# Cross attention's output projection computed in pairs of token tiles from seven block products, and the last unit's later sums taken by TensorE with ones

## The chip, the cores and the metric

One core of one Trainium2 chip runs the whole kernel in one launch. The metric is the device time of that launch in microseconds (us), the median of three runs. TensorE (PE) does the matrix products, VectorE (DVE) and ScalarE (ACT) the elementwise work, GpSimd (POOL) elementwise work in SBUF and some transfers, SyncE (SP) issues most of the transfers.

## The reference, cut to what matters

One block of a perceiver on 16 batches of 64 latent tokens (1024 tokens in all, 1024 wide, float32). Three residual steps follow each other; the change lies at the end of the first.

```python
x = x + xattn(layernorm(x), ctx, ctx, Wq, Wk, Wv, Wo)   # context: 16 x 1024 x 1024
x = x + attn(layernorm(x), wq, bq, wk, bk, wv, bv)      # rotary, no output projection
x = x + ffn(layernorm(x), w_gate, w_up, w_down)         # int4 / int8 / ternary rounding

def xattn(query, key, value, Wq, Wk, Wv, Wo):           # 32 heads of 32, 8 key/value heads
    ...
    scores = einsum('bhqd,bhkd->bhqk', q, k) * 32 ** -0.5
    probs = softmax(scores)
    out = einsum('bhqk,bhkd->bqhd', probs, v).reshape(b, sq, 1024)
    return out @ Wo                                     # 1024 x 1024
```

## The kernel before

**Tiles.** The 1024 tokens are 8 token tiles of 128, tile t holding batches 2t and 2t+1. Almost everything in SBUF lies in one tile, the `arena`; `place(kb, shape)` is a view of it that begins at that kilobyte of each partition, and the same kilobytes serve several tensors one after the other. All engine queues run in the order in which the code emits the work (a manual schedule), so an instruction that waits holds up everything behind it on its engine.

**Cross attention** is 32 units: unit n is batch n // 2 with key/value heads 4g to 4g+3, g = n % 2. A loop over n = 0 to 31 with an inner loop over i = 0 to 3 interleaves the stages of neighbouring units. Called "step (n, i)" below, a step emits in this order:

- `by_key` of unit n+1 (line 696): scores of a quarter of the keys into the two PSUM tiles w0 and w1; ScalarE copies them to SBUF (line 708), VectorE keeps running maxima (lines 712, 715). At i = 3 `reduce` (lines 720 to 727) finds the maxima over keys and `spread` (lines 733, 734) writes them to DRAM and reads them back to all partitions through SP's queue.
- loads on SP's queue that are tied to that step (token tiles x, outputs of earlier batches, weights).
- `fill(2)`: two pieces from the list `fillers`, which hold projection work for TensorE. A second `fill` follows later in the step.
- at i = 1 and 2, `exponentials` of unit n: VectorE subtracts the maxima (line 739, 128x2048), ScalarE takes the exponential (line 740), and `sums` on GpSimd adds up the keys into `acc` (lines 746, 749).
- at i = 0, `values((2, 3))` of unit n-1 (line 758) and `finish` (line 768, four products of `ones` with `acc`, one for each group of 32 columns); at i = 1 its `quotients` on VectorE (lines 777 to 787). At i = 2, `values((0, 1))` of unit n.

In the last pass, n = 31, there is no following unit, and all exponentials and sums of unit 31 are emitted in it.

**The output projection** `project_out(t, h)` (lines 258 and 798) makes one half of 512 columns of one token tile: eight products of 128x128 weights with 512 moving columns into one PSUM bank (a filler has two of them), then one VectorE addition onto the token tile `xs[t]`. There are 16 of these. Tile (4, 0) is filler of step (29, 3), tiles 5, 4, 0 and 1 are fillers of passes 30 and 31, and tiles 2, 3, 6 and 7 follow after the loop, with the normalization `norm2` (lines 179 to 193) and the transposes `transpose2` (lines 296 to 300) of the next attention among them. After that comes `project2`, whose first product is the k projection (line 258, name k).

Outputs of batches 0 to 11 were kept in DRAM (`results`) and are loaded into `outputs[t]` before their projection; those of the last two tiles stay in SBUF, and tile 7 is only complete after unit 31's `quotients`.

`bank(n, name)` names a PSUM bank: 0 and 1 are m0 and m1, 2 is t1.

The order of SP's queue in passes 29 to 31 follows the code: the maxima's write and read of `spread`, then the loads listed after it. A load waits in the queue until its target kilobytes are free, and holds up those behind it.

Of the kernel before, what the change touches and what calls it, by code (L numbers as in the profile page):

```python
# [20 lines left out]
P = 128  # L21
# [28 lines left out]
def kernel(  # L50
# [148 lines left out]
    early = [place(16 * half, [4, 2, 2, 4, NQ]) for half in range(2)]  # L199
    two_tiles = [place(4 * i, [2, 2, 4 * NQ]) for i in range(2)]  # L200
    two_outputs = [place(4 * i, [2, 4, 2, NQ]) for i in range(2)]
    outputs = [place(8 + 4 * t if t < 6 else 4 * (t - 6), [2, 4, P]) for t in range(NT)]

    qa = [place(16 * g, [B * 4 * NQ]) for g in range(2)]
    queries = [a.rearrange("p (b r q) -> p b r q", r=4, q=NQ) for a in qa]
# [23 lines left out]
    def load_x(dst, t):  # L229
        nc.sync.dma_start(dst, x[bass.ts(t, P), :])  # L230

    def load(src):
        st = stream.next([KC, 512])
        nc.sync.dma_start(st, src)
        return st

    def load_half(h, i):
        if i == 0:
            wos.append(stream.next([KC, 512]))
        part = slice(4 * i, 4 * i + 4)  # L240
        nc.sync.dma_start(wos[h][:, part], wo[h][:, part])

    def load_queries(st, src, engine, pieces):

# [5 lines left out]
    def matmul_steps(out, lhsT, rhs, done, pieces=2):  # L250

        made = []

        def piece(i):
            if i == 0:
                made.append(out())
            for k in range(i * KC // pieces, (i + 1) * KC // pieces):
                nc.tensor.matmul(  # L258
                    made[0], lhsT=lhsT(k), rhs=rhs(k), start=(k == 0), stop=(k == KC - 1)
                )  # L260
# [421 lines left out]
    class Unit:  # L682
# [80 lines left out]
                            stop=(kt == 7),  # L763
                        )

        def finish(self):
            for jj in range(4):
                nc.tensor.matmul(
                    self.po[bass.ts(jj, HD), 256:512],
                    lhsT=ones,  # L770
                    rhs=acc[:, jj, :],
                    start=True,
                    stop=True,
                )

        def quotients(self):
            nc.vector.reciprocal(rs, self.po[:, 256:512])
# [9 lines left out]
                nc.gpsimd.tensor_copy(view[:, :, 0, :], split(aside[self.g]))  # L787


    wos = []  # L790

    def project_out(t, h):
        cols = bass.ts(h, 512)
        return matmul_steps(
            lambda: m_tile(f"wo_{t}_{h}"),
            lambda k: outputs[t][:, k // 4, k % 4, :],
            lambda k: wos[h][:, k, :],
            lambda ps: nc.vector.tensor_tensor(xs[t][:, cols], ps, xs[t][:, cols], ALU.add),
            pieces=4,
        )  # L800


    n2T = [[place(kb, [4, 512]) for kb in kbs] for kbs in ((136, 144), (48, 56))]
    n2_ring = Ring(180, 176)
    n2s = {}
    kT2 = place(112, [2, B, NQ])
    v2 = place(120, [NT, KVD])
    oS = place(152, [2, 4, 2, NQ])
    sS = place(156, [4, 2, NQ])

# [5 lines left out]
    turned_ring = Ring(168, 170)  # L816
    rope_sb = place(192.25, [2 * NQ])
    bv_sb = place(192.75, [KVD])
    wkvs2 = place(32, [KC, 512])
    wqs2 = []  # L820
    swap = [(i + HD // 2) % HD for i in range(HD)]

    def norm2(t):
        n2s[t] = n2_ring.next([DIM])
        for step in layernorm(n2s[t], xs[t], f"n2_{t}"):
            step()

    def transpose2(t, tile):
        half, tl = t // 4, t % 4
        cols = bass.ts(tl, P)  # L830
        transposed([a[:, :, cols] for a in n2T[half]], n2s[t], f"n2p_{t}", tile, ("act", "dve"))
# [189 lines left out]
    inter = [  # L1021
        place(kb, [INTER]) for kb in (48, 58.75, 69.5, 80.25, 0, 10.75, 136, 146.75)
    ]
    wb_ring = Ring(32, 34.6875, 37.375, 40.0625, 91.25, 42.75)
    relu_ring = Ring(45.4375, 192.25, 199.625)
    prod_ring = Ring(172.5, 174)
    wds = [place(112 + c if c < 16 else 6 + c, [DIM], F8) for c in range(NIC)]
    q_ring = Ring(157.5, 162.875)
    qT_ring = Ring(48, 59)
    xq3 = {}  # L1030
# [95 lines left out]
    def fetch_down():  # L1126
        wd_rows = ternary_d.rearrange("c p f -> (c p f)").rearrange("(i h) -> i h", h=DIM)
        nc.gpsimd.memset(wds[NIC - 1][LAST:], 0.0)
        for c0, c1 in ((0, 16), (16, NIC - 1)):
            nc.sync.dma_start(  # L1130
                place(112 if c0 == 0 else 22, [c1 - c0, DIM], F8),
                wd_rows[c0 * P : c1 * P].rearrange("(c p) h -> p c h", p=P),
            )
        nc.sync.dma_start(wds[NIC - 1][:LAST], wd_rows[(NIC - 1) * P :])
# [43 lines left out]
    def fill(n=1):  # L1178
        for _ in range(n):
            if fillers:  # L1180
                fillers.pop(0)()

    with tc.manual_schedule():
# [45 lines left out]
        for n in range(2 * B):  # L1229

            b = n // 2
            if n % 2 == 0:
                if n == 2:
                    weight_sum(1, 0)
                fill(len(fillers))
                if b == 0:
                    load_context(1, 1)
                    kT, v, key_steps, value_steps = project(1)
                    for h in range(2):

                        for step in key_steps[h] + value_steps[h]:
                            fillers += [step, lambda: None]
                    begun = project_fast(2)
                    early = begun[2]
                    fillers[-3], fillers[-1] = early[:2]
                    fillers += early[2:]
                elif b + 1 < B:
                    kT, v, early_steps, steps = begun
                    fillers += steps
                    begun = project_fast(b + 2) if b + 2 < B else None  # L1250
                    if begun:
                        fillers += begun[2]
                    else:
                        fillers += project_out(4, 0)
                if b + 1 < B:
                    tiles.append((kT, v))
                else:
                    for t in range(4):
                        load_x(xs[t], t)
                    for t, h in ((5, 0), (4, 1), (5, 1)):  # L1260
                        fillers += project_out(t, h)
                    for t in (0, 1):
                        for h in range(2):
                            fillers += project_out(t, h)
            following = Unit(n + 1, *tiles[(n + 1) // 2]) if n + 1 < 2 * B else None

            for i in range(4):
# [6 lines left out]
                if n == 5 and i == 3:  # L1274
                    nc.vector.tensor_reduce(tot, asum, AX.X, ALU.add)
                if n == 2 * B - 4 and i in (0, 3):
                    load_half(0, i // 3)
                if n == 2 * B - 3 and i == 2:
                    for k in range(2):
                        load_half(1, k)  # L1280
                if i == 1 and n == 2 * B - 2:
                    nc.sync.dma_start(wkvs2, wkv2)

                fast, odd = 1 <= b < B - 1, n % 2
                if n == 0 and i == 3:
# [22 lines left out]
                        nc.sync.dma_start(place(4 * (t % 2), [DIM]), spilled[t + 2])  # L1308
                for when, ts in (
                    ((2 * B - 3, 2), (4, 5)),  # L1310
                    ((2 * B - 3, 3), (2, 3)),
                    ((2 * B - 2, 1), (0, 1)),
                ):
                    for t in ts if when == (n, i) else ():
                        nc.sync.dma_start(outputs[t].rearrange("p g r c -> p (g r c)"), results[t])
# [13 lines left out]
                    unit.sums(1)  # L1329
                if i == 3 and held_back:  # L1330
                    unit.sums(3)
                fill(0 if i == 0 and fast or (n, i) == (6, 2) else 2)
                if i == 1 and held_back:
                    unit.sums(0)
                if last and i == 0:
# [11 lines left out]
                if i == 1 and not following:  # L1347
                    for e in (2, 3):
                        unit.exponentials(e)
                        unit.sums(e)  # L1350
# [4 lines left out]
                if i == 3 and not following:  # L1355
                    unit.values((2, 3))
# [8 lines left out]
        for t in (2, 3):  # L1365
            for h in range(2):
                fillers += project_out(t, h)
                if t == 2:
                    fillers += [lambda h=h: norm2(h)]
            fillers += [lambda t=t: (transpose2(t - 2, m_tile), norm2(t))]  # L1370
        fill(9)
        last.finish()
        last.quotients()
        fill(len(fillers))
        for h in range(2):
            fillers += project_out(6, h)
        fillers += [lambda: transpose2(2, m_tile)]
        for h in range(2):
            fillers += project_out(7, h)
        fill(len(fillers))  # L1380
        transpose2(3, m_tile)
# [189 lines left out]
```

## Time and profile before

| what | number |
| --- | --- |
| median of 3 runs | 1823.31 us (1818.98 to 1824.83) |
| the profiled execution, its own time | 1819.01 us |
| its span in the profile | 1817.2 us |
| mean granted TensorE clock | 0.995 of full speed |
| output projection, line 258 name wo | 256 records, 114.2 us busy |
| the additions of its results, line 798 | 16, 10.9 us busy |

The profile's times are from the start of the span. One float32 product appears as two records of TensorE, so the 256 records are 128 products. A row of the timeline gives the start, the duration, the engine, line, operation, names and shapes, the number of records merged, and in brackets how long the engine was idle before it and who ended that.

### The profile page before, as it was taken

To read this page: it belongs to the slowest core of one execution; us is meant where nothing else is said; L and a number is where in the kernel's file an instruction comes from. 1 tells how busy PE (TensorE), PEld (TensorE's weight loads), DVE (VectorE), ACT (ScalarE), POOL (GpSimd) and SP (SyncE) were. 2 spreads that over 40 slices of the span, in tenths; PEclk is the share of its full clock that TensorE was granted. 3 is DMA by queue.
4 is the path that set the end of the run, shared out by engine and by line. 5 is a ranking of instruction groups with operands and counts; after the bars stand their busy time and mean duration, and the time that the engine had idled before them with its cause. 6 is when DMAs were issued, how large, how long until landed. Compare 5 with 4: busy or idle time off the path is not lost.

```text
span 1817.2 us, 29757 instructions
## 1 busy us (share of the span) xinstructions
PE 1771.3 (97%) x12424; PEld 1139.4 (63%) x12424; DVE 1252.5 (69%) x1500; ACT 946.6 (52%) x1034; POOL 937.7 (52%) x568
## 2 busy tenths in 40 slices
PE   8999999999999999999999999999999998999999
PEld 5887576666667667667667667654346454566654
DVE  4343778778888888878888888877423367675554
ACT  1563666656677777777677665543101122763221
POOL 1000447657767667767767767664403425455510
PEclk9999999999999999999999999999999999999999
DMA  9566457576677777677777766353020022333201
GB/s 355 165 224 216 181 168 210 158 195 192 193 206 198 232 213 208 216 211 205 221 204 215 217 187 168 92 194 143 5 93 0 6 73 63 84 105 112 73 30 53
DMA packets 67735, 285.52 MB, mean 157 GB/s; under 512 B 10576, under 2 KB 19728, under 8 KB 52880
## 3 DMA queue, kind: packets, MB, share of 16 engines
q1 hardware_dynamic: 54288, 213.63, 32.9%
q0 software_dynamic: 12160, 67.89, 18.4%
q8 instruction: 98, 1.61, 0.3%
q10 hardware_dynamic: 1152, 2.10, 0.3%
q14 instruction: 37, 0.30, 0.1%
HBM read 264.38 MB, written 19.20 MB: 156 GB/s over the span
## 4 chain that ended last, share of the span: by engine, by line
PE 83%; DVE 8%; DMA 4%; ACT 3%; POOL 2%; issue 1%; ACTq 0%; DVEq 0%; POOLq 0%
PE p L514 14%; PE p L503 13%; PE t L696 7%; PE o L758 6%; PE q L366 5%; PE q L258 5%; PE wo L258 4%; PE d L1161 4%; PE k L258 4%; PE g L1082 4%; PE gu L1082 3%; DVE arena L739 3%; DMA arena<-in_ctxT 3%; PE z L514 3%; PE v L427 2%; DVE arena L715 2%
## 5 line engine op out<-in xcount | busy, mean ns | idle before, releaser
L749 POOL TENSOR_TENSOR arena<-arena 128x1024 f32<-128x1024 f32 x192 | 506.5, 2638 | 78.5 <-ACT arena L740 63.5
L715 DVE TENSOR_TENSOR arena<-t,arena 128x512 f32<-128x512 f32 x384 | 261.2, 689 | 171.3 <-PE t L696 105.0
L739 DVE TENSOR_TENSOR arena<-arena 128x2048 f32<-128x2048 f32 x128 | 358.8, 2833 | 6.8 <-DMA arena<-tops 6.8
L740 ACT ACTIVATE arena<-arena 128x2048 f32<-128x2048 f32 x128 | 244.1, 1907 | 186.7 <-DVE arena L739 186.5
L514 PEld LDWEIGHTS p<-arena 128*128 128x128 f32 x2688 | 311.5, 193 | 34.0 <-issue 25.7
L708 ACT COPY arena<-t 128x1024 f32<-128x1024 f32 x256 | 253.4, 1009 | 144.5 <-DVE arena L712 62.5
L514 PE MATMUL p<-arena 128*128 128x128 f32 x2688 | 319.7, 277 | 0.0
L503 PE MATMUL p<-arena 128*128 128x512 f32 x672 | 307.5, 599 | 7.3 <-DMA arena<-in_ctxT 7.3
L503 PEld LDWEIGHTS p<-arena 128*128 128x128 f32 x672 | 121.7, 190 | 149.9 <-issue 138.1
L746 POOL TENSOR_TENSOR arena<-arena 128x1024 f32<-128x1024 f32 x32 | 75.6, 2363 | 271.1 <-ACT arena L740 194.5
L696 PE MATMUL t<-arena 32*128 32x256 f32 x2048 | 146.7, 400 | 5.5 <-ACT arena L708 3.3
L1082 PEld LDWEIGHTS <-arena 128*128 128x128 bf16 x1024 | 98.8, 98 | 64.8 <-issue 13.7
L696 PEld LDWEIGHTS t<-arena 32*128 32x128 f32 x2048 | 93.0, 184 | 63.9 <-issue 32.6
L758 PE MATMUL o<-arena 128*32 128x256 f32 x2048 | 124.8, 384 | 4.1 <-ACT arena L740 3.8
L258 PE MATMUL wo<-arena 128*128 128x512 f32 x256 | 114.2, 603 | 0.3 <-ACT arena L298 0.3
L258 PE MATMUL q<-arena 128*128 128x512 f32 x256 | 112.6, 595 | 0.0
L843 POOL TENSOR_TENSOR arena<-arena 128x512 f32<-128x512 f32 x20 | 33.5, 1673 | 133.9 <-DVE arena L841 133.9
L366 PE MATMUL q<-arena 128*128 128x256 f32 x448 | 99.1, 380 | 1.3 <-ACT arena L377 1.3
L758 PEld LDWEIGHTS o<-arena 128*32 128x32 f32 x2048 | 60.3, 110 | 57.5 <-ACT arena L646 6.8
L1082 PE MATMUL gu<-arena 128*128 128x344 fp8e4 x544 | 85.4, 314 | 9.6 <-ACT arena L1090 6.5
L366 PEld LDWEIGHTS q<-arena 128*128 128x128 f32 x448 | 84.2, 190 | 14.4 <-issue 1.7
L483 POOL DMA_DIRECT2D arena<-in_ctxT x70 | 69.4, 1047 | 40.1 <-PE z L514 17.2
(158 smaller groups left out, 2340.0 us busy)
## 6 DMA issues: line engine op xcount, KB each, us to landing
arena<-in_ctxT SPq DMA_DIRECT2D x56, 1024.0 KB, 10.3
arena<-in_ctxT POOLq DMA_DIRECT2D x42, 1024.0 KB, 10.7
arena<-tops SPq DMA_DIRECT2D x48, 512.0 KB, 4.8
arena<-in_wg SPq DMA_DIRECT2D x32, 688.0 KB, 5.1
arena<-in_wu SPq DMA_DIRECT2D x32, 688.0 KB, 5.5
arena<-in_wd SPq DMA_DIRECT2D x32, 688.0 KB, 8.3
arena<-in_ctxT POOLq DMA_DIRECT2D x28, 512.0 KB, 8.4
arena<-ternary POOLq DMA_DIRECT2D x26, 344.0 KB, 3.8
```

What stands on the lines that cost most here:

```text
L258: nc.tensor.matmul(made[0], lhsT=lhsT(k), rhs=rhs(k), start=(k == 0), stop=(k == KC - 1))
L366: nc.tensor.matmul(ps, lhsT=weights[:, k, :], rhs=what[:, k, :], start=(start and k == 0), stop=(k == 3), skip_group_check=True,)
L503: nc.tensor.matmul(ps, lhsT=weights[:, k, :], rhs=what[:, k, :], start=(first and k == 0), stop=(k == 3), skip_group_check=True,)
L514: nc.tensor.matmul(ps[:, bass.ts(kt, P)], lhsT=what[:, k, bass.ts(kt, P)], rhs=weights[:, k, :], start=(first and kt == 0 and k == 0), sto ...
L696: nc.tensor.matmul(ws[jj // 2][:, jj % 2, a, :], lhsT=self.kT[rows, self.g, bass.ts(i * 2 + a, P)], rhs=two_tiles[self.b // 2 % 2][rows, s ...
L708: nc.scalar.copy(pt[:, 2 * mine : 2 * mine + 2], ws[mine])
L715: nc.vector.tensor_tensor(m, w[:, :, a], m, ALU.max)
L739: nc.vector.tensor_tensor(pt, pt, by.to_broadcast([P, 4, 2, 256]), ALU.subtract)
L740: nc.scalar.activation(pt, pt, AF.Exp)
L749: nc.gpsimd.tensor_tensor(acc, acc, pt[:, :, a], ALU.add)
L758: nc.tensor.matmul(self.po[bass.ts(jj, HD), 0:256], lhsT=self.v[:, kt, bass.ts(self.g * 4 + jj, HD)], rhs=self.pts[i][:, jj, a, :], start= ...
L1082: nc.tensor.matmul(ps[:, :CW], lhsT=xqT[t][:, k, :], rhs=wbs[n][i][:, k, :], start=(k == 0), stop=(k == KC - 1),)
```

## The change

Two neighbouring token tiles t and t+1, each cut into two halves of the contraction (512 input rows), make a 2x2 block matrix a11, a12 (tile t) and a21, a22 (tile t+1). `Wo` is a 2x2 block matrix too (`out_blocks`). `project_out(t, turn)` now makes a pair of tiles from seven block products instead of eight. Their operands include sums: `sum_out` makes three sums of weight blocks once (and overwrites b12), `sum_pair` four sums of token blocks for each pair (one overwrites a21), all on VectorE. Four of the products accumulate in one bank (`turn` 0 or 1), one after the other, and after each of them VectorE adds what the bank holds to a quarter of the pair; the other three share bank 2. A filler is two of a product's four matrix products. Pairs go in the order (4, 5), (0, 1), (2, 3), (6, 7).

The last unit's sums of its third and fourth quarter of the keys leave GpSimd; `finish((2, 3))` lets TensorE multiply those probabilities with `ones` and accumulate. Loads move between steps, some tensors move to other kilobytes, the transposes of tiles 0 to 3 use w0 and w1, and step (30, 0) runs two fillers instead of four.

```diff
-    outputs = [place(8 + 4 * t if t < 6 else 4 * (t - 6), [2, 4, P]) for t in range(NT)]
+    outputs = [place(kb, [2, 4, P]) for kb in (8, 12, 196, 24, 24, 28, 0, 4)]
...
-        def finish(self):
+        def finish(self, direct=()):
+            rest = [(i, a) for i in direct for a in range(2)]
             for jj in range(4):
-                nc.tensor.matmul(
-                    self.po[bass.ts(jj, HD), 256:512],
-                    lhsT=ones,
-                    rhs=acc[:, jj, :],
...
+                rows = [acc[:, jj, :]] + [self.pts[i][:, jj, a, :] for i, a in rest]
+                for n, row in enumerate(rows):
+                    nc.tensor.matmul(
+                        self.po[bass.ts(jj, HD), 256:512],
+                        lhsT=ones,
+                        rhs=row,
+                        start=(n == 0),
+                        stop=(n == len(rows) - 1),
+                    )
...
+    def sum_out(n):
+        (b11, b12), (b21, b22) = out_blocks
+        t1, t2, t4 = out_sums
+        out, a, b, op = (
+            (b12, b22, b12, ALU.subtract),
+            (t2, b12, b11, ALU.add),
+            (t1, b22, t2, ALU.subtract),
+            (t4, b21, t2, ALU.subtract),
+        )[n]
+        nc.vector.tensor_tensor(out, a, b, op)
...
+    def sum_pair(t, ns):
+        (a11, a12), (a21, a22) = pair_blocks(t)
+        s1, s2, s4 = pair_sums[t]
+        sums = (
+            (s1, a21, a22, ALU.add),
+            (s2, s1, a11, ALU.subtract),
+            (a21, a11, a21, ALU.subtract),
+            (s4, a12, s2, ALU.subtract),
         )
+        for n in ns:
+            nc.vector.tensor_tensor(*sums[n])
+
+    def project_out(t, turn):
...
+        def product(n, first, what, weights, *adds):
+            def piece(i):
+                if i == 0 and first:
+                    held[n] = bank(n, f"wo_{t}_{n}")
+                for k in (2 * i, 2 * i + 1):
+                    nc.tensor.matmul(
+                        held[n],
...
+                for h, g in adds if i else ():
+                    dst = xs[t + h][:, bass.ts(g, 512)]
+                    nc.vector.tensor_tensor(dst, held[n], dst, ALU.add)
...
+        begin = product(turn, True, a11, b11, (0, 0)) + product(2, True, a12, b21, (0, 0))
+        rest = product(turn, False, s2, t2, (0, 1)) + product(2, True, s1, t1, (1, 1))
+        rest += product(turn, False, s3, t3, (1, 1)) + product(2, False, s4, b22, (0, 1))
+        return begin, rest + product(turn, False, a22, t4, (1, 0))
...
-                        fillers += project_out(4, 0)
+                        pairs = {t: project_out(t, turn % 2) for turn, t in enumerate((4, 0, 2, 6))}
+                        fillers += pairs[4][0]
...
+                    for a, b_ in ((0, 4), (2, 0), (6, 2)):
+                        fillers += pairs[a][0] + pairs[b_][1]
+                    fillers += pairs[6][1]
...
+                if (n, i) == (2 * B - 3, 3):
+                    for t in (0, 1):
+                        load_x(xs[t], t)
+                    sum_out(0)
+                    sum_out(1)
+                if (n, i) == (2 * B - 2, 0):
+                    sum_pair(4, (0, 1))
+                if (n, i) == (2 * B - 2, 1):
+                    sum_out(2)
+                    sum_pair(4, (2,))
+                if (n, i) == (2 * B - 2, 2):
+                    sum_pair(4, (3,))
+                    sum_out(3)
+                if (n, i) == (2 * B - 1, 0):
+                    load_x(xs[2], 2)
+                    sum_pair(0, range(4))
...
                     ((2 * B - 3, 2), (4, 5)),
-                    ((2 * B - 3, 3), (2, 3)),
-                    ((2 * B - 2, 1), (0, 1)),
+                    ((2 * B - 3, 3), (0, 1)),
+                    ((2 * B - 2, 1), (2,)),
+                    ((2 * B - 1, 0), (3,)),
                 ):
                     for t in ts if when == (n, i) else ():
                         nc.sync.dma_start(outputs[t].rearrange("p g r c -> p (g r c)"), results[t])
...
-                fill(0 if i == 0 and fast or (n, i) == (6, 2) else 2)
+                fill(0 if i == 0 and b or (n, i) == (6, 2) else 2)
...
+        load_x(xs[3], 3)
+        sum_pair(2, (0, 1))
+        fill(4)
+        last.values((2, 3))
+        last.finish((2, 3))
+        nc.sync.dma_start(wkvs2, wkv2)
+        last.quotients()
+        sum_pair(2, (2, 3))
+        fill(4)
+        norm2(0)
+        norm2(1)
+        sum_pair(6, range(4))
+        fill(2)
+        transpose2(0, wide_tile)
+        fill(2)
...
```

Below, a block product is named by its operands, for example s1·t1. Emitted into the queues, the fillers fall as follows: step (29, 3) has a11·b11 and a12·b21 of pair (4, 5); step (30, 0) a11·b11 of pair (0, 1); step (30, 1) a12·b21 of pair (0, 1) and s2·t2 of pair (4, 5); step (30, 2) s1·t1 and s3·t3, step (30, 3) s4·b22 and a22·t4, all of pair (4, 5). Pass 31 has a11·b11 (step 0) and a12·b21 of pair (2, 3), then the five later products of pair (0, 1). After the loop come a11·b11 and a12·b21 of pair (6, 7), unit 31's last `values` and `finish`. Ten products remain after `finish`, the five later ones of pairs (2, 3) and (6, 7).

More of the change, by code (lines that the diff above doesn't have):

```diff
@@ L235, in load @@
         return st
[L237 to L241, printed above, removed]
     def load_queries(st, src, engine, pieces):
@@ L764, in values @@
                         )
-        def finish(self):
+        def finish(self, direct=()):
+            rest = [(i, a) for i in direct for a in range(2)]
             for jj in range(4):
-                nc.tensor.matmul(
-                    self.po[bass.ts(jj, HD), 256:512],
-                    lhsT=ones,
-                    rhs=acc[:, jj, :],
-                    start=True,
-                    stop=True,
-                )
+                rows = [acc[:, jj, :]] + [self.pts[i][:, jj, a, :] for i, a in rest]
[7 more added lines that the diff above has]
+                    )
         def quotients(self):
@@ L787, in quotients @@
                 nc.gpsimd.tensor_copy(view[:, :, 0, :], split(aside[self.g]))
[L790 to L799, printed above, removed]
-        )
+    out_blocks = [[place(kb, [4, 512]) for kb in kbs] for kbs in ((64, 16), (72, 32))]
@@ new lines, with load_out @@
+    out_sums = [place(kb, [4, 512]) for kb in (88, 80, 40)]
+    pair_places = {4: (104, 106, 108), 0: (172, 174, 110), 2: (8, 10, 12), 6: (28, 30, 14)}
+    pair_sums = {t: [place(kb, [4, P]) for kb in kbs] for t, kbs in pair_places.items()}
+    def load_out(i, h):
+        nc.sync.dma_start(out_blocks[i][h], wo[h][:, 4 * i : 4 * i + 4])
+    def sum_out(n):
[8 more added lines that the diff above has]
+        nc.vector.tensor_tensor(out, a, b, op)
@@ new lines, in pair_blocks @@
+    def pair_blocks(t):
+        return [[outputs[t + h][:, i] for i in range(2)] for h in range(2)]
+    def sum_pair(t, ns):
[6 more added lines that the diff above has]
+            (s4, a12, s2, ALU.subtract),
+        )
+        for n in ns:
+            nc.vector.tensor_tensor(*sums[n])
+    def project_out(t, turn):
+        (a11, a12), (s3, a22) = pair_blocks(t)
+        s1, s2, s4 = pair_sums[t]
+        (b11, t3), (b21, b22) = out_blocks
+        t1, t2, t4 = out_sums
+        held = {}
+        def product(n, first, what, weights, *adds):
[5 more added lines that the diff above has]
+                        held[n],
+                        lhsT=what[:, k, :],
+                        rhs=weights[:, k, :],
+                        start=(first and k == 0),
+                        stop=(k == 3),
+                        skip_group_check=True,
+                    )
+                for h, g in adds if i else ():
+                    dst = xs[t + h][:, bass.ts(g, 512)]
+                    nc.vector.tensor_tensor(dst, held[n], dst, ALU.add)
+            return [lambda: piece(0), lambda: piece(1)]
+        begin = product(turn, True, a11, b11, (0, 0)) + product(2, True, a12, b21, (0, 0))
+        rest = product(turn, False, s2, t2, (0, 1)) + product(2, True, s1, t1, (1, 1))
+        rest += product(turn, False, s3, t3, (1, 1)) + product(2, False, s4, b22, (0, 1))
+        return begin, rest + product(turn, False, a22, t4, (1, 0))
@@ L805 @@
     n2s = {}
-    kT2 = place(112, [2, B, NQ])
-    v2 = place(120, [NT, KVD])
+    kT2 = place(32, [2, B, NQ])
+    v2 = place(40, [NT, KVD])
     oS = place(152, [2, 4, 2, NQ])
@@ L818 @@
     bv_sb = place(192.75, [KVD])
-    wkvs2 = place(32, [KC, 512])
+    wkvs2 = place(112, [KC, 512])
     wqs2 = []
@@ L1023 @@
     ]
-    wb_ring = Ring(32, 34.6875, 37.375, 40.0625, 91.25, 42.75)
-    relu_ring = Ring(45.4375, 192.25, 199.625)
+    wb_ring = Ring(112, 114.6875, 117.375, 120.0625, 91.25, 122.75)
+    relu_ring = Ring(125.4375, 192.25, 199.625)
     prod_ring = Ring(172.5, 174)
-    wds = [place(112 + c if c < 16 else 6 + c, [DIM], F8) for c in range(NIC)]
+    wds = [place(32 + c if c < 16 else 6 + c, [DIM], F8) for c in range(NIC)]
     q_ring = Ring(157.5, 162.875)
@@ L1130, in fetch_down @@
             nc.sync.dma_start(
-                place(112 if c0 == 0 else 22, [c1 - c0, DIM], F8),
+                place(32 if c0 == 0 else 22, [c1 - c0, DIM], F8),
                 wd_rows[c0 * P : c1 * P].rearrange("(c p) h -> p c h", p=P),
@@ L1257 @@
                 else:
[L1258 to L1264, printed above, removed]
+                    for a, b_ in ((0, 4), (2, 0), (6, 2)):
+                        fillers += pairs[a][0] + pairs[b_][1]
+                    fillers += pairs[6][1]
             following = Unit(n + 1, *tiles[(n + 1) // 2]) if n + 1 < 2 * B else None
@@ L1276 @@
                 if n == 2 * B - 4 and i in (0, 3):
[L1277 to L1282, printed above, removed]
+                    load_out(i // 3, 0)
+                if n == 2 * B - 3 and i in (0, 1):
+                    load_out(1 - i, 1)
+                if (n, i) == (2 * B - 3, 3):
[14 more added lines that the diff above has]
+                    sum_pair(0, range(4))
                 fast, odd = 1 <= b < B - 1, n % 2
@@ L1349 @@
                         unit.exponentials(e)
-                        unit.sums(e)
                 if (n, i) == (6, 2):
@@ L1354 @@
                     unit.values((0, 1))
-                if i == 3 and not following:
-                    unit.values((2, 3))
             if n == 2 * B - 4:
@@ L1363, with wide_tile @@
             last, unit = unit, following
-        fill(len(fillers))
[L1365 to L1381, printed above, removed]
+        def wide_tile(name):
+            turns["m"] ^= 1
+            w = ps_w.tile([P, 2, 2, 256], F32, tag=f"w{turns['m']}", name=name)
+            return w.rearrange("p a b c -> p (a b c)")[:, 0:512]
+        load_x(xs[3], 3)
[13 more added lines that the diff above has]
+        fill(2)
+        transpose2(1, wide_tile)
+        fill(2)
+        norm2(2)
+        fill(2)
+        norm2(3)
+        fill(2)
+        transpose2(2, wide_tile)
+        fill(2)
+        transpose2(3, wide_tile)
+        fill(len(fillers))
         nc.sync.dma_start(rope_sb, rope)
```

## The prediction

> **What bounds the kernel now.** I read the page first, then the chain of waits, then the timelines of TensorE, VectorE and SP around the projection.
>
> ```profile
> PE 1771.3 (97%) x12424; PEld 1139.4 (63%) x12424; DVE 1252.5 (69%) x1500; ACT 946.6 (52%) x1034; POOL 937.7 (52%) x568
> ```
>
> TensorE is the bound of the whole, but an average says nothing on this stage. The chain of waits there:
>
> ```profile
> 1217.35 7.06 PE wo L258 x16
> ...
> 1227.79 7.08 PE wo L258 x16
> 1234.89 0.69 DVE arena L798
> 1235.58 3.81 DVE arena L739
> ...
> 1259.45 1.33 DMA tops<-arena
> 1260.80 4.20 DMA arena<-tops
> ```
>
> In pass 30 the chain changes from TensorE to VectorE and to the maxima's transfer and back: VectorE is within a microsecond or two of being the bound itself. The work of each engine by window (PE, PEld, DVE, ACT, POOL busy, then TensorE's granted clock) says the same:
>
> ```profile
> 1226.00:1262.00 36.00, 36.00 (x200) 16.36 (x190) 28.64 (x29) 13.40 (x10) 17.13 (x7) 1.00 0.35 145
> 1262.00:1300.00 38.00, 34.23 (x132) 14.63 (x128) 19.38 (x14) 7.66 (x4) 21.69 (x10) 0.91 0.12 41
> ```
>
> In pass 30 (first row) TensorE has no gap and VectorE 7.4 us free. TensorE's timeline:
>
> ```profile
> 1217.28 7.13 PE L258 MATMUL wo<-arena 128*128 128x512 f32 x16
> 1224.35 1.93 PE L758 MATMUL o<-arena 128*32 128x256 f32 x32
> 1226.10 0.61 PE L768 MATMUL o<-arena,ones 128*32 128x256 f32 x8
> ...
> 1262.09 14.00 PE L258 MATMUL wo<-arena 128*128 128x512 f32 x32
> ...
> 1282.79 1.94 PE L758 MATMUL o<-arena 128*32 128x256 f32 x16 [3.25 <-ACT arena L740]
> 1284.66 15.78 PE L258 MATMUL wo<-arena 128*128 128x512 f32 x32
> ```
>
> The one long wait (3.25) is for the last exponential. After it the same 32 records take 15.78 instead of 14.00, where the window's clock is 0.91: a long wait costs 1.8 us more behind it. SP and VectorE:
>
> ```profile
> 1219.94 0.33 SPq L734 DMA_DIRECT2D arena<-tops  x1
> ...
> 1221.27 2.25 SPq L230 DMA_DIRECT2D arena<-in_x  x4
> ```
>
> ```profile
> arena<-in_x SPq DMA_DIRECT2D x1, 512.0 KB, 6.8
> ```
>
> The second fence is the DMA view of the transfer issued at 1221.27, the fourth of 512 KB from 1219.94 on: it landed 6.8 later, at 1228.1.
>
> ```profile
> 1265.09 4.49 DVE L739 TENSOR_TENSOR arena<-arena 128x2048 f32<-128x2048 f32 x2 [4.47 <-DMA arena<-tops]
> ...
> 1272.23 8.57 DVE L739 TENSOR_TENSOR arena<-arena 128x2048 f32<-128x2048 f32 x2
> ```
>
> Two such subtractions take 4.49 when GpSimd is idle, 8.57 while it adds: whichever comes second stands still until the other is done.
>
> **Part 1, fewer products.** Before: 8 tiles x 2 halves x 8 = 128. After: 4 pairs x 7 x 4 = 112. 32 records (16 products) take 14.00, so 16 fewer save 14.0 us, all on TensorE's path.
>
> **Part 2, `finish` of unit 31.** 4 products with ones become 20. Below: groups of four in four column groups take 0.61 (row L768), five groups 3.05. Above: one 128x256 product after another (line 366, 99.1 us for 224) is 0.442 each, 20 make 8.8. The new order has five products in a row on the same 32 columns and the same PSUM rows, so I go by line 366 and, as row L768 has different groups side by side, let the last of one group run beside the first of the next: 17 x 0.442 = 7.5, +6.9 over the 0.6 before.
>
> The Trainium skill ("TensorE: Matmul & The Clock Gate", Part 3, packing small matmuls) says that products run side by side when they are in different column groups and that they start and end in order, which speaks against this order; no row here shows five in one group. By that rule the sum stands as it is, by row L768 it would be 4.5 us lower.
>
> The four GpSimd additions that go (2.35 each) ran from 1281.0 to 1290.6, and `finish` came at 1300.4 without a wait: nothing on the path.
>
> **Part 3, the new waits.** I walked the queues by hand from step (29, 3): an instruction starts when its engine is free and its inputs are there, with durations from the rows (additions from PSUM 0.69, 128x512 sums in SBUF 0.69 as line 346, 128x2048 sums 2.28 as line 739, more where GpSimd is in the way). The same walk over the order before puts the first k product at 1348.4; the trace has 1348.25.
>
> - Step (30, 0): TensorE reaches a11·b11 of pair (0, 1) at 1217.3 (by_key begins at 1216.2, as now). Its operand, tile 0's outputs, is loaded behind `spread` and tiles xs[0] and xs[1] on SP. `spread` can't go before the maxima are reduced (1218.5), so the load is issued at 1221.3, fourth behind the broadcast, and lands at 1228.1 as the row above did. Wait 10.8 us. Before, tile 5 stood here, loaded 20 us earlier. Queued behind it: unit 29's last values and `finish`, and the next by_key. VectorE makes the first two weight sums meanwhile (4.6 us, from 1218.4), which the wait hides; without it they would hold by_key up by 3.5.
> - Step (30, 3): s4·b22 needs bank 2, so the addition of s1·t1, which stands on VectorE behind s4's sum and the fourth weight sum. VectorE is through with the maxima at 1252.9, loses 2.2 to GpSimd, and ends s4's sum at 1255.8, the weight sum at 1258.2, the addition at 1258.8. TensorE was free at 1254.9: 3.9 us.
> - Step (31, 0): a11·b11 of pair (2, 3) takes over bank 0 from pair (4, 5). The bank's last addition is emitted after `reduce`, which begins after the last maxima (1268.2) and ends at 1271.9; then two additions to 1273.2. TensorE was free at 1267.6: 5.6 us.
> - VectorE's addition of that product goes onto xs[2], whose load SP issues behind the broadcast, xs[6] and xs[7], landing about 8.2 after the broadcast's issue (4.2, then 1.3 for each of three, 0.1 for the order): 1281.5. The subtraction behind it waits 4 us longer than for the broadcast itself; the four products ahead on TensorE cover it. But later, at step (31, 3), s4·b22 of pair (0, 1) wants bank 2, whose addition stands behind two subtractions slowed by GpSimd (3.4 and 4.5): 1299.3 against 1296.9, 2.4 us.
> - a11·b11 of pair (6, 7) takes bank 1 from pair (0, 1): 0.9. Tiles 0 and 1 transposed: 0.4 for the norm, 1.7 because the copy stands behind sum_pair of (6, 7) and an addition.
>
> Together 10.8 + 3.9 + 5.6 + 2.4 + 0.9 + 0.4 + 1.7 = 25.7. The first three waits are longer than 3 us, so each gets 1.8 of slow clock: 5.3.
>
> **Part 4, what goes.** Waits of 0.5 and 3.3 for the last exponentials (now ten us of products lie between), 1.3 before transposes, 1.8 of slow clock: 6.9.
>
> **What costs nothing.** The sums of weights and tokens not named above, and 28 instead of 16 additions (12 x 0.69 = 8.3), fall into VectorE's gaps; in pass 30 there is no such cover, and that is where the waits come from. wkv is issued behind `finish` (1323.6), 10.4 us to land as now, needed at 1365; were the cover gone, the k product would wait. xs[3] lands at 1308, needed at 1330. The second attention's weights stand behind wkv on SP and have 30 us of k and v products as cover.
>
> **Sum.** -14.0 + 6.9 + 25.7 + 5.3 - 6.9 = +17.0 us. On the profiled execution, 1819.0 + 17.0 = 1836.0; on the median, which is 4.3 above it, 1840.3. I take the middle, 1838. This measurement can tell 0.3%, 5.5 us, from no change. Between the two bases (1821.2) the cases are:
>
> **The rivals.**
> - *TensorE runs through* (faster): VectorE's additions and sums fit its gaps, so that no bank is handed over late and tile 0 is there in time. Place: the bank hand-overs of passes 30 and 31. Price: -14.0 + 6.9 - 6.9 = -14, about 1807. It decides as soon as the new waits and slow clock stay under 14 us against my 31. For it: 69% average use of VectorE. Against: 7.4 free in pass 30, into which more than 15 go. 0.06.
> - *Tile 0's outputs land in time*: the walk without that wait has by_key of step (30, 1) held 3.5 by the weight sums, bank 0 at (31, 0) 7.3, and ends at +10: 1831. Against: the 1228.1 of the row. 0.10.
> - *`finish` runs four abreast*: 3.05 instead of 7.5: +12.5, 1834. 0.15.
> - *VectorE falls further behind*, each short sum held once by a GpSimd addition (2.4) and the clock slow after every wait: +6 on top, 1844. 0.08.
> - Parts cancel within 0.3%: 0.03. That the change isn't what it says I exclude: the queues hold 28 block products and 20 products with ones.
>
> **How the numbers follow.** My forecast has 0.58. With `finish` from 3.05 to 8.8 (-4.5, +1.3), slow clock from none to four times (some 1.7 either way) and the base from 1819.0 to 1824.8 it reaches from 1830 to 1846; the second to fourth rival lie in 1828 to 1847, which leaves out the first, the fifth and some of the tails, under 0.2. Faster 0.06, same 0.03, slower 0.91.
>
> **What would show it.** In the timeline after: TensorE waiting about 10.8 us for `results` after by_key of step (30, 0); waits for VectorE's addition of an earlier product of some 4 and 6 us in steps (30, 3) and (31, 0); a row of 40 records with ones of about 7.5 us; k starting 17 us later than 1348; nothing different after that. Wrong if the first wait is under 3 us, or if k starts before 1350.

## The result and the profile after

The changed kernel takes 1842.2 us (median, 1840.81 to 1843.57) against 1822.07 for the kernel before on the same chip: slower by 1.1%, ratio 1.0111 [1.0092, 1.013] (in brackets its 95% interval). The profiled execution took 1840.81 us, its span is 1839.0 us, 21.8 more than the span of before.

The page of the changed kernel, busy time of each engine:

```profile
PE 1770.3 (96%) x12424; PEld 1139.7 (62%) x12424; DVE 1276.8 (69%) x1532; ACT 945.8 (51%) x1034; POOL 926.2 (50%) x564
```

TensorE is busy 1.0 us less than before, VectorE 24.3 more, while the span is 21.8 longer. So most of what the saved products take off TensorE comes back on it as something else (the products with ones and a lower clock, below), and the added time is TensorE waiting. The number of TensorE records is the same by coincidence (32 fewer of `wo`, 32 more with `ones`). The two windows that the prediction read, now in the changed kernel (columns as there: PE, PEld, DVE, ACT, POOL busy, granted clock, DMA share, GB/s):

```profile
1226.00:1262.00 36.00, 29.74 (x164) 13.63 (x165) 28.74 (x28) 9.34 (x8) 8.14 (x3) 0.88 0.12 50
1262.00:1300.00 38.00, 29.69 (x126) 12.71 (x125) 29.59 (x30) 11.68 (x8) 22.34 (x9) 0.94 0.20 70
```

Where TensorE had no gap in pass 30 it now stands for 6.3 us, and 8.3 in the next window; the longest wait, which ends at 1228.79, lies mostly ahead of the first. The chain of waits has the three that count, the first two by what ended them, the third by the products that stand behind it:

```profile
1221.98 6.76 DMA arena<-results
1228.79 5.48 PE wo L833 x8
...
1254.25 4.36 DVE arena L804
...
1273.61 5.26 PE wo L833 x8
```

L804 is `sum_out`. TensorE's timeline, the rows behind a wait, the row of the last unit's products with ones, and the first k product:

```profile
1228.79 5.48 PE L833 MATMUL wo<-arena 128*128 128x512 f32 x8 [11.05 <-DMA arena<-results]
...
1259.26 8.83 PE L833 MATMUL wo<-arena 128*128 128x512 f32 x16 [3.47 <-DVE arena L843]
1273.61 5.26 PE L833 MATMUL wo<-arena 128*128 128x512 f32 x8 [5.52 <-DVE arena L843]
...
1299.75 8.83 PE L833 MATMUL wo<-arena 128*128 128x512 f32 x16 [2.79 <-DVE arena L843]
1309.36 7.13 PE L833 MATMUL wo<-arena 128*128 128x512 f32 x16 [0.78 <-DVE arena L843]
1318.18 6.30 PE L765 MATMUL o<-arena,ones 128*32 128x256 f32 x40
...
1366.11 13.97 PE L252 MATMUL k<-arena 128*128 128x512 f32 x32 [0.83 <-issue]
```

Undisturbed, 8 records of this shape take 3.70 and 16 take 7.13: the four rows above that take 5.48, 8.83, 5.26 and 8.83 ran at a lower clock. The granted clock over them is 0.67, 0.81, 0.70 and 0.81, and 1.00 over the row of 1309.36. I measure the stage from here on from the first `wo` product to the first k product: 1348.25 - 1209.14 = 139.1 us before, 1366.11 - 1209.53 = 156.6 after, 17.5 more. In the stage TensorE is busy 129.8 us against 134.0 before and idle 26.8 against 5.1.

Why the waits end when they do is on the other engines. SP's queue and VectorE of the changed kernel:

```profile
1219.20 0.32 SPq L727 DMA_DIRECT2D tops<-arena  x1
1220.55 0.32 SPq L728 DMA_DIRECT2D arena<-tops  x1
1220.92 0.90 SPq L230 DMA_DIRECT2D arena<-in_x  x2
1221.98 1.58 SPq L1376 DMA_DIRECT2D arena<-results  x3
```

```profile
1254.16 4.44 DVE L804 TENSOR_TENSOR arena<-arena 128x2048 f32<-128x2048 f32 x1
1258.53 0.68 DVE L843 TENSOR_TENSOR arena<-wo,arena 128x512 f32<-128x512 f32 x1
...
1272.00 0.36 DVE L721 TENSOR_REDUCE arena<-arena 32x32 f32<-32x128 f32 x1
1272.29 1.26 DVE L843 TENSOR_TENSOR arena<-wo,arena 128x512 f32<-128x512 f32 x2
```

Tile 0's outputs are issued behind `spread` (L727 and L728) and two token tiles. The addition that gives bank 2 free stands behind the fourth weight sum, which GpSimd stretches from 2.28 to 4.44; the additions that give bank 0 free (1272.29) stand behind the last instruction of `reduce` (1272.00).

### The profile page after: what moved, and what is told of

It is laid out like the page before. It is cut to its first block, busy times and chain, and to the rows that moved or that the text cites. A ratio compares the mean times of both kernels' runs of the same rounds, so it can differ in the third digit from the quotient of the medians.

```text
span 1839.0 us, 29793 instructions
## 1 busy us (share of the span) xinstructions
PE 1770.3 (96%) x12424; PEld 1139.7 (62%) x12424; DVE 1276.8 (69%) x1532; ACT 945.8 (51%) x1034; POOL 926.2 (50%) x564
## 4 chain that ended last, share of the span: by engine, by line
PE 77%; DVE 11%; DMA 5%; issue 3%; ACT 3%; POOL 1%; SPq 0%; ACTq 0%; DVEq 0%; POOLq 0%
PE p L508 14%; PE p L497 12%; PE t L690 6%; PE o L752 6%; PE q L360 5%; PE q L252 5%; PE d L1211 4%; PE k L252 4%; DVE arena L733 4%; PE wo L833 3%; PE g L1132 3%; PE z L508 3%; DMA arena<-in_ctxT 3%; DVE arena L709 2%; PE v L421 2%
## 5 line engine op out<-in xcount | busy, mean ns | idle before, releaser
L743 POOL TENSOR_TENSOR arena<-arena 128x1024 f32<-128x1024 f32 x188 | 495.8, 2637 | 78.1 <-ACT arena L734 63.1
L733 DVE TENSOR_TENSOR arena<-arena 128x2048 f32<-128x2048 f32 x128 | 354.4, 2798 | 1.0 <-DMA arena<-tops 1.0
L740 POOL TENSOR_TENSOR arena<-arena 128x1024 f32<-128x1024 f32 x32 | 76.7, 2397 | 289.0 <-ACT arena L734 226.7
L497 PEld LDWEIGHTS p<-arena 128*128 128x128 f32 x672 | 121.7, 190 | 148.2 <-issue 137.0
L833 PE MATMUL wo<-arena 128*128 128x512 f32 x224 | 106.2, 630 | 23.6 <-DVE arena L843 12.6
L833 PEld LDWEIGHTS wo<-arena 128*128 128x128 f32 x224 | 43.9, 201 | 79.5 <-issue 52.2
```

The lines of the kernel that those rows point to most:

```text
L497: nc.tensor.matmul(ps, lhsT=weights[:, k, :], rhs=what[:, k, :], start=(first and k == 0), stop=(k == 3), skip_group_check=True,)
L733: nc.vector.tensor_tensor(pt, pt, by.to_broadcast([P, 4, 2, 256]), ALU.subtract)
L743: nc.gpsimd.tensor_tensor(acc, acc, pt[:, :, a], ALU.add)
```

## The experiments

All stages below are from the first `wo` to the first k product; "ratio" is against runs of the kernel before on the same chip, beside which each kernel was run. The kernel before had a median of 1822.07 beside the changed kernel, 1822.51 beside e1 to e4, 1821.23 beside e5 to e7 and 1823.4 beside e9 and e10.

| kernel | stage us | median us | ratio |
| --- | --- | --- | --- |
| before, two profiles | 139.1 and 138.1 | 1822.07 | 1 |
| changed | 156.6 | 1842.2 | 1.0111 [1.0092, 1.013] |
| e2, ones across groups | 152.8 | 1837.11 | 1.0074 [1.005, 1.0099] |
| e3, before and part 2 alone | 143.9 | 1826.87 | 1.0023 [1.0005, 1.004] |
| e4, no sums | 149.0 | 1833.59 | 1.0051 [1.0033, 1.0068] |
| e5, loads earlier | 148.2 | 1832.54 | 1.006 [1.004, 1.0079] |
| e6, e5 and e2 | 145.2 | 1828.79 | 1.0037 [1.0026, 1.0049] |
| e7, rearranged | 130.3 | 1812.92 | 0.9956 [0.9942, 0.9971] |
| e9, rearranged, t4 in time | 132.2 | 1815.27 | 0.9961 [0.9946, 0.9975] |
| e10, e9 with GpSimd | 130.9 | 1815.62 | 0.9959 [0.9943, 0.9976] |

**The wait for tile 0, first try (e1).** The loads go into the list of step (29, 2).

```diff
-                    ((2 * B - 3, 2), (4, 5)),
-                    ((2 * B - 3, 3), (0, 1)),
+                    ((2 * B - 3, 2), (4, 5, 0, 1)),
```

> The loads of tiles 0 and 1's outputs move from step (29, 3) to step (29, 2), ahead of the maxima's write on SP's queue; all else as after. Theory (the new waits in passes 30 and 31 cost more than the saved products): the wait of 11.05 us before a11*b11 of pair (0, 1) and its slow clock go, but VectorE's first two weight sums, then without cover, hold by_key of step (30, 1) up by some 3.5 us; the first k product starts 7 to 9 us earlier than after (1366.1), so about 1358, and the time falls by as much, to about 1834. Rival (VectorE is so far behind that the wait only stood in for others): less than 2 us earlier. Rival (the wait is all there is): 12.8 us earlier.

Median 1837.65 us, ratio 1.0086 [1.0056, 1.0117]. The 11.05 before a11·b11 was gone, but TensorE waited 8.09 for `results` one step earlier: in the order of the code the loads now stood ahead of batch 15's last value products, which therefore took these kilobytes as their operand (that part of the computation is changed) and waited for them. The wait had moved, not gone, and the expectation failed: k started at 1371.0, not at about 1358. (The wait now lies ahead of the first `wo` product, so the stage says nothing here, and e1 isn't in the table.) Behind it by_key of step (30, 1) waited 3.69 as expected.

**The products with ones, in another order (e2).** The loop over the terms goes outside, the loop over the four column groups inside.

```diff
-            for jj in range(4):
-                rows = [acc[:, jj, :]] + [self.pts[i][:, jj, a, :] for i, a in rest]
-                for n, row in enumerate(rows):
+            for n in range(len(rest) + 1):
+                for jj in range(4):
+                    ...
```

> Unit 31's 20 products with ones are emitted row by row over the four column groups instead of column group by column group; all else as after. Theory (products in one column group follow each other, those in four run side by side): the row of 40 records falls from 6.30 us to 2.75 to 3.05 (five times 0.55 to 0.61), k starts 3.3 us earlier than after. Rival (the order makes no difference, each accumulation waits for the one before): 6.3 us as now, k within 0.3 us of after.

The row in TensorE's timeline of e2:

```profile
1321.49 2.34 PE L769 MATMUL o<-arena,ones 128*32 128x256 f32 x40
```

The same 40 records take 2.34 instead of 6.30 when neighbours are in different column groups, and the stage is 3.8 shorter (1365.47 - 1212.64 = 152.8): nothing of the saving came back as a wait. I had expected 2.75 to 3.05; five rounds over the four groups cost less than five single ones of 0.55 to 0.61.

**Part 2 alone on the kernel before (e3).** `finish` and the last unit's sums as changed, the output projection as before.

> The kernel before with part 2 alone: the last unit's sums of its third and fourth quarter by TensorE with ones, 20 products in the changed kernel's order, and four GpSimd additions fewer. Theory (those GpSimd additions were off the path, the products are on it): k starts 5.6 us later than before's 1348.25, the row with ones takes 6.3 us. Rival (GpSimd's additions stood in VectorE's way and held the last exponentials back): the wait of 3.25 us before the last values and the 1.8 us of slow clock behind it go too, k starts within 1 us of before.

Stage 143.9, 4.8 more than the profile of before and 5.9 more than a second profile of it (e8). The row with ones takes 6.32 instead of 0.64. k itself starts at 1352.62, 4.4 later than in before, where I had said 5.6; most of the difference is the `wo` row behind the wait, 14.76 here and 15.78 there. The wait of 3.25 before the last values is still there, so the GpSimd additions that part 2 takes away were worth nothing here, and part 2 is between a quarter and a third of the stage's loss.

**No sums at all (e4).** Neither weight nor token sums are made; the products read what lies in those kilobytes.

```diff
-        nc.vector.tensor_tensor(out, a, b, op)
+        pass
...
-            nc.vector.tensor_tensor(*sums[n])
+            pass
```

> The changed kernel without VectorE's 4 weight sums and 16 token sums: the products run on operands that were never summed, so the output isn't the reference's; products, additions, loads and their order are all as after. Theory (VectorE's queue makes part of the waits, the load and the bank order the rest): the waits of 3.47 us before s4*b22 and of 1.87 us before a transpose go, the wait of 11.05 us for the load and most of the 5.52 us at step (31, 0) stay; k starts 5 to 8 us earlier than after. Rival (the sums fall into gaps of VectorE and cost nothing): within 1 us of after. Rival (VectorE's extra work is the whole loss): k starts 15 us or more earlier.

Stage 149.0, 7.6 less. The waits of 3.47 and 1.87 are gone, those of 10.79 (load) and 6.25 (bank 0 behind `reduce`) stay: the sums cost what stands behind them in VectorE's queue, and the two longest waits have other causes. Of the 7.6, 5.0 are waits and 2.3 the lower clock behind waits; 1.7 of that stands behind the wait at step (31, 3), which is still there (2.62) but was followed by full speed this time, so it can't be put down to the sums.

**The loads between (e5).** At the end of step (29, 2), behind the value products and still ahead of `spread`.

```diff
-                    ((2 * B - 3, 3), (0, 1)),
...
+                if (n, i) == (2 * B - 3, 2):
+                    for t in (0, 1):
+                        nc.sync.dma_start(outputs[t].rearrange("p g r c -> p (g r c)"), results[t])
                 if last and i == 0:
```

> The outputs of tiles 0 and 1 are loaded at the end of step (29, 2), behind the last value products of batch 15 that read those kilobytes, and ahead of the maxima's write and read of step (29, 3) in SP's queue; else the kernel is the changed one. The stage is measured from the first wo product to the first k product: 139.1 us before, 156.6 after. Theory (walk of the queues): the wait of 11.05 for results goes and nothing takes its place in front of it; the first two weight sums then hold by_key of step (30, 1) by some 3.5; the waits of 3.5, 5.5, 2.8, 0.8, 0.5 and 1.9 stay: stage 148.7, 7.9 less than after, median about 1834. Rival (the load only hid VectorE's lag, which comes out in full): TensorE waits 4.6 or more for by_key and longer at both bank hand-overs, stage above 152. Second rival (the wait moves onto another transfer, as in the first try with the loads ahead of the value products): a wait of 6 us or more that a DMA ends, stage above 153.

Two rows of e5's TensorE timeline:

```profile
1233.82 2.09 PE L690 MATMUL t<-arena 32*128 32x256 f32 x16 [4.76 <-DVE arena L706]
...
1272.02 5.75 PE L833 MATMUL wo<-arena 128*128 128x512 f32 x8 [7.22 <-DVE arena L843]
```

The 11 us wait is gone and the stage is 8.4 shorter, not 11: by_key now waits 4.76 for VectorE (L706 is its first maxima, behind the weight sums; the walk said 3.5), and the hand-over of bank 0 grows from 5.5 to 7.2. The load had hidden work of VectorE, as the prediction had it. Of the first rival's signs, the wait of 4.6 for by_key came and the hand-over of bank 0 took longer, but that of bank 2 took less (2.25 instead of 3.47) and the stage stayed under 152. Of the 8.4, 2.4 come from the clock, which stayed at full speed behind two of the waits; e6, set against e2, takes the same step and gains 7.6.

**Both together (e6).**

> As e5, and the ones products of the last unit go round the four column groups (row by row, then group by group within the row). Theory: the two savings add, since the products with ones stand on TensorE alone: row of 40 records 2.3 us, stage 144.8 (11.8 less than after, 5.7 more than before), median about 1830. Rival (VectorE decides there too: norm2 of tile 0 and the sums of pair (6, 7) are then late): half of the 4 us comes back as longer waits before the transposes, stage 146.8 or more.

Stage 1354.67 - 1209.48 = 145.2. The two savings add to within 0.8 (3.8 + 8.4 = 12.2, measured 11.4), and the projection is still 6 to 7 us longer than before although TensorE has 14 us less of `wo` products in it. What is left are waits for VectorE, 4.75, 2.38, 5.51, 2.61, 0.78, 0.46 and 1.87, and 6.9 us of lower clock behind them.

**The order of VectorE's work (e7).** As e6; the 28 products come in another order, and each sum has its own place, found with the walk of the queues.

```diff
+    late_products = (
+        "01 43 02 44 45 47 46 03 62 05 04 07 21 06 61 22 23 24 25 26 27 63 64 65 66 67"
+    )
+    sums_at = {
+        (29, 3, 0): ((4, 0),),
+        (29, 3, 1): ((None, 0), (4, 1), (0, 0)),
+        ...
+    }
...
-                    for a, b_ in ((0, 4), (2, 0), (6, 2)):
-                        fillers += pairs[a][0] + pairs[b_][1]
-                    fillers += pairs[6][1]
+                    for name in late_products.split():
+                        fillers += pairs[int(name[0])]["p" + name[1]]
```

"43" is product 3 (s2·t2) of pair (4, 5); in `sums_at` the entry (4, 0) is that pair's first sum, (None, 0) the first weight sum, and the key is a step and a place in it.

> As e6, with the products of the four pairs in another order (the additions in front of a bank hand-over have one or two other products between), the weight and token sums each at the step where VectorE is free by the walk, and the sums of pair (6, 7) later among the norms. The arithmetic is the same 28 block products, 20 products with ones and 20 sums. Theory (VectorE's place in the queue at four points is the whole cost, not its amount of work): waits of some 2.8 before by_key of step (30, 1), 2.3, 1.3 and 2.1 in front of products, none above 3 us, stage 130.6, 8.5 less than before, median about 1816, ratio 0.995 to 0.997. Rival (VectorE has too much work in pass 30 wherever it stands): waits there still sum to 10 or more, stage 137 or above, no better than before.

Stage 1341.46 - 1211.20 = 130.3, ratio 0.9956. TensorE waits 3.43 before by_key of step (30, 1), where I had said 2.8 and nothing above 3, then 1.31, 1.77 and 0.52. The order of the products and the places of the sums and norms changed together, so what each is worth alone isn't shown. In this kernel t4 is made behind the product of pair (4, 5) that reads it, which changes that product's operand; its instructions are all there. So its time could owe something to the sum that came too late, and e9 repairs that.

**The kernel before, once more (e8).**

> The kernel before once more, for its profile. Theory: the stage from the first wo product to the first k product is the same from profile to profile within 0.5 us (139.1), while what lies ahead of it (first wo at 1208.7 to 1212.9 so far) and behind it (469 to 473) differs by several us between profiles, so the 3.9 us by which the changed kernel's profile is longer behind k is no part of the change. Rival (the part behind k is fixed for a kernel): 469.0 within 0.3 here, and 472.9 belongs to the change.

Stage 138.1, 1.0 less than the other profile of before, where I had said 0.5. Most of it is clock: behind the same wait (3.26 and 3.25) the values and the `wo` products take 1.07 + 15.70 here and took 1.94 + 15.78. Behind k the span is 471.5 here and was 469.0. The changed kernel has 472.9, and the other kernels, which are the same there, lie between 468.8 and 475.9: the 3.9 us behind k are within what profiles differ by.

**All sums in time (e9 and e10).** e9 makes t4 at step (30, 1); e10 in addition gives t2 and t1 to GpSimd in halves.

```diff
-        "01 43 02 44 45 47 46 03 62 05 04 07 21 06 61 22 23 24 25 26 27 63 64 65 66 67"
+        "01 43 02 45 44 03 46 47 62 05 04 07 21 06 61 22 24 23 26 25 27 63 64 65 66 67"
...
-        (31, 0, 0): ((None, 3),),
+        (30, 1, 0): ((None, 3), (4, 2),),
```

> The rearranged kernel in an order in which every sum stands ahead of the product that reads it (in e7 the weight sum t4 stood behind the last product of pair (4, 5)): t4 is now made at step (30, 1), in the pass in which VectorE has least room, the sums of pairs (4, 5) and (0, 1) are spread further, the order of products differs a little. Theory (walk): waits of 2.8 before by_key of step (30, 1), 1.7 before s2*t2, 0.7 and 1.0 in front of products of pair (4, 5), 0.9 before by_key of (30, 3), 2.8 before finish of unit 30 and 0.6, 0.5 behind it, none above 3; stage 132.8 from the first wo to the first k product (138.1 to 139.1 before, 156.6 in the changed kernel, 130.3 in e7), median about 1815, ratio 0.996 to 0.998. Rival (e7 owed its gain to the sum that it made too late): the 2.3 us of t4 and the additions behind it come back in full and with slow clock, stage 136 or above, median within 0.2% of before.

> As e9, with the weight sums t2 and t1 on GpSimd, each in two halves, in the 15 us of pass 30 in which GpSimd has nothing to do, and another order of products. Theory (walk, with GpSimd and VectorE taking turns in SBUF): waits of 3.2 before by_key of (30, 1), 0.5 before s1*t1, 2.5 before finish of unit 30; stage 130.8, median about 1813, ratio 0.995 to 0.997. Rival (GpSimd's halves hold up VectorE's short sums, which then hand over a bank late, as sum_out(0) took 3.6 and sum_out(3) 4.4 us instead of 2.3 in the changed kernel): waits before s2*t2 and s1*t1 of 2 to 4 us and slow clock, stage 135 or above, not better than e9.

e9's waits in TensorE's timeline:

```profile
1227.57 2.09 PE L690 MATMUL t<-arena 32*128 32x256 f32 x16 [3.46 <-DVE arena L706]
1230.36 8.72 PE L837 MATMUL wo<-arena 128*128 128x512 f32 x16 [0.71 <-DVE arena L808]
...
1254.70 7.13 PE L837 MATMUL wo<-arena 128*128 128x512 f32 x16 [0.82 <-DVE arena L823]
...
1266.43 0.64 PE L769 MATMUL o<-arena,ones 128*32 128x256 f32 x8 [2.73 <-POOL arena L743]
1267.58 15.70 PE L837 MATMUL wo<-arena 128*128 128x512 f32 x32 [0.51 <-DVE arena L847]
```

Stage 1342.13 - 1209.97 = 132.2 (132.8 expected), waits 8.2 in all instead of 26 (the walk had 11.0, and none above 3). It beats both kernels: 1815.27 us, ratio 0.9961 [0.9946, 0.9975], with the same products, sums and additions as the changed kernel. Its rival falls: the gain of e7 was not owed to the late sum. So does that of e7: VectorE is busy 100.3 us in this stage and 101.8 in the changed kernel's, so its amount of work was not what made the changed kernel slower. e10 has the stage of the walk too (1341.91 - 1211.04 = 130.9), though its waits are not those of the walk (4.41, 1.38 and 2.36 instead of 3.2, 0.5 and 2.5), and cannot be told from e9 in time. Its rival shows in part: a token sum that takes 0.68 alone is held by GpSimd's halves, and TensorE waits 1.38 behind it.

```profile
1229.45 2.86 DVE L828 TENSOR_TENSOR arena<-arena 128x512 f32<-128x512 f32 x1
```

## Why the prediction was right, point by point

- **Direction and mechanism.** Slower, by three new waits, each where it was put: 11.05 (10.8), 3.47 (3.9) and 5.52 (5.6). The smaller ones are 2.79, 0.78, 0.47 and 1.87 (2.4, 0.9, 0.4, 1.7). Together 25.95 against 25.7. e5 shows the first one's cause, e4 the second's, e9 that the third goes when other products stand between the bank's last addition and its next use. Neither taking out the sums nor moving the loads nor the order of the products with ones ends the third (6.25 in e4, 7.22 in e5, 5.51 in e6).
- **Fewer products.** -14.0 held: with 1.7 more of products with ones (2.34 - 0.64), 8.2 of waits, 4.2 of slow clock (2.09, 8.72 and 15.70 instead of 1.15, 7.13 and 14.00) and the 6.9 that goes, e9 should stand at -6.8; its stage is 5.9 to 6.9 under before.
- **`finish`.** Mis-sized: the row measured 6.30 and not 7.5 (+5.7, not +6.9). The order was rightly read (five products in a group follow each other), the price of one was not: 6.30 over the 17 that follow each other is 0.37, and 0.442 from line 366 was too high. The rival "four abreast" was wrong for this order; in e2's order it was right, and its 3.05 still above the 2.34 measured.
- **Slow clock.** Mis-sized the other way: four rows instead of three, 1.78 + 1.70 + 1.56 + 1.70 = 6.7 instead of 5.3. The wait of 2.79 was followed by a lower clock too.
- **The sum of the stage.** -14.0 + 5.7 + 25.95 + 6.7 - 6.9 = +17.5, measured +17.5, predicted +17.0: the two wrong sizes (-1.2 and +1.4) nearly cancel, which is luck. Two more terms were missing and cancel too: the 0.83 of "issue" before k, and 0.87 that goes, since in the profile of before the last 16 records of values behind the wait of 3.25 took 1.94 (granted clock 0.50) and the 16 ahead of it 1.07.
- **Time.** 1842.2 against 1838, inside the range. Of the 4.2 the stage explains 0.5, and 0.9 is the base: I added to 1821.2, the middle of the profile's own time and the median, and the kernel before took 1822.07 beside this one. Apart from rounding, about 2.6 are left: the medians differ by 20.1 and the stage by 17.5. The interval of the ratio allows 16.8 to 23.7, so this may be spread between runs. "Nothing different after k" was wrong for that one profile (3.9 longer), which e8 and the others show to be spread between profiles. Ahead of the stage the first `wo` product starts at 1208.7 to 1209.1 in three profiles with the old projection and at 1209.5 to 1214.9 in eight with the new one (all but e1, whose wait lies ahead of it). The means, 1208.9 and 1211.5, lie about 2.6 apart, though the changed kernel's own profile has 1209.5; whether the change has a part in this stays open.
- **The range.** Its clock term is too narrow below: no slow clock at all would take off 5.3 and not 1.7. Above, its parts add up to 1844.8 and not 1846. The result lies inside either way.
- **"VectorE falls further behind"** did not come, "TensorE runs through" neither: even rearranged, 8 us of waits were left.

## What to carry to other kernels

Here fewer products helped only when the engine that makes their operands and empties their banks came to them in time: e9 and the changed kernel have the same work, and the order in which it is emitted (loads, sums, products, products with ones) separates 1.1% slower from 0.4% faster. When a chain of products shares a bank, look at what is emitted on the emptying engine between the last addition and the bank's next product. When a wait is removed, look first at what it was hiding (11 us removed gave 7.6 to 8.4).

## What the runs showed of the hardware

Twenty products with ones take 6.30 us one column group after the other and 2.34 group by group in turn. The Trainium skill ("TensorE: Matmul & The Clock Gate", Part 3, packing small matmuls) says that products whose outputs lie in different column groups of the array run side by side; the two rows agree.

The lower clock behind a wait does not go by the wait's length alone. The wait at step (31, 3) was followed by slow products in e6 and by products at full speed in e4, where it was no shorter:

```profile
1292.27 8.83 PE L837 MATMUL wo<-arena 128*128 128x512 f32 x16 [2.61 <-DVE arena L847]
```

```profile
1299.27 7.13 PE L833 MATMUL wo<-arena 128*128 128x512 f32 x16 [2.62 <-DVE arena L843]
```

In e2 (2.61) it was 8.83 too, in e5 (2.60) 7.13 too; the granted clock over the 4.4 us behind it was 0.66 in e6 and 1.00 in e5. The windows behind two other waits, the first of 2.38 us in e6, the second of 2.25 us in e5 (the granted clock is the third number from the right):

```profile
1251.68:1256.10 4.42, 4.42 (x7) 1.88 (x8) 4.42 (x3) 1.91 (x1) 0.19 (x1) 0.62 0.01 2
```

```profile
1257.67:1262.10 4.43, 4.43 (x11) 2.04 (x12) 4.43 (x3) 1.91 (x1) 0.20 (x1) 1.00 0.01 2
```

The Trainium skill ("TensorE: Matmul & The Clock Gate", Part 1, the clock gate) puts the fall to half speed behind an idle window of about 3.4 us, and says that the window runs freely. Shorter waits (2.38 and 2.61) were enough here, so the measurement goes before the figure; a window that runs freely would explain why the same wait costs 1.7 us in one profile and nothing in another, but no run here shows the window itself.
